# One middle stage of a four-layer kernel: ScalarE put into program order, and the two pairs of batches one turn apart instead of four

## The chip, the cores and the metric

The kernel runs on one core of a Trainium2 chip. A core has five engines that work beside each other and meet through semaphores: TensorE (PE in the profile; PEld is its weight load), VectorE (DVE), ScalarE (ACT), GpSimd (POOL) and SyncE (SP, which here only starts DMA transfers). What is measured is the device time of one execution in microseconds (us); the time of a version is the median of several runs.

## The reference, cut to what matters

Four batches of 512 tokens with 128 features, in float32, pass through four "macaron" layers. Each layer adds half a feed-forward part, an attention part and again half a feed-forward part, each on the normalized x:

```python
x = x + 0.5 * ffn(layernorm(x))
x = x + attn(layernorm(x))
x = x + 0.5 * ffn(layernorm(x))
```

The layers differ in what `ffn` and `attn` are. The change lies between the end of the second layer's attention and the experts of the fourth layer's first feed-forward part. Five parts are computed there:

1. Second layer's second `ffn`: eight small experts with `silu(x wg) * (x wu)`, then `wd`, of which each token uses two with weights made from sigmoid scores, and a shared expert that all tokens use.
2. Third layer's first `ffn`: eight linear experts (`x w_in w_out`), of which each token uses two, with a softmax over the two largest logits.
3. Third layer's `attn`, which is a recurrence: a projection of x to a gate and a hidden part, `g = sigmoid(gate) * silu(hidden)`, then along the tokens `h = 0.9 h + 0.1 g`, then an output projection.
4. Third layer's second `ffn`: as part 2, with the same weights, on the new x.
5. Fourth layer's first `ffn`, its beginning alone: logits, a softmax, the two best experts of each token, and the place of each token among the 512 that an expert takes. The tokens are scattered to those places in DRAM, and the experts then fetch them. In the traces this part is "the third mixture" (f30), the first two being those of the first layer.

## The kernel before, in words

x stays in SBUF for the whole run, in four tiles `xs[b]` of 128 partitions x 4 token tiles x 128 features, one for each batch. Weights of the third layer's experts are folded beforehand: `w_in w_out` of each expert is one 128x128 matrix, all eight in a tile `m`. So one token tile of 128 tokens needs two matmuls of 128x512 (L1419) for all its experts, and VectorE then adds the eight products, each times the gate of its token, to x (L1450, a gating product: 32 for each batch and part, 256 in all).

The stage works on two pairs of batches, 0 and 1, 2 and 3. One Python generator, `behind`, emits the five parts for one pair and yields between steps, and `skewed` takes the generators in turns. The second generator joins in after `lag` turns:

```python
def skewed(gens, lag):
    live = {i: g for i, g in enumerate(gens)}
    r = 0
    while live:
        for i in list(live):
            if r >= i * lag and next(live[i], "end") == "end":
                del live[i]
        r += 1
        yield
```

So the order of the program is a few instructions of pair one, a few of pair two, and so on. What the engines get is not this order for all of them. A planner orders the instructions of each engine by priorities and its own notion of when each is ready. `tc.manual_schedule(engines=...)` takes engines out of that: what is emitted for them inside the block stays in the order of the program. Before the change only GpSimd is in that set here; TensorE, VectorE and ScalarE are ordered by the planner, and SyncE too. Every engine then executes its own list strictly in order, so an instruction that waits holds up all behind it.

The steps, with the lines that the profile names:

- Each part begins with the norm. Statistics on VectorE (L168, L169, one each for every token tile), then GpSimd makes `rs` (L172), `rstd` (L173) and, where ScalarE normalizes, `off` (L176, L177). Normalizing runs on ScalarE (L182) and VectorE (L186), half of the token tiles each in parts 1 to 4; for the third mixture it is all on ScalarE. TensorE transposes (L195), ScalarE copies the result to `nT` (L1124; L321 for the mixture).
- Gate logits: small matmuls (L1133; L330 for the mixture). Routing on VectorE: largest value, one-hot, the rest, the second one (L226 to L239).
- Part 1 (`l1_ffn`): a gu pair of matmuls (L1218, L1219) for each of five blocks of 128 hidden units and each batch; sigmoid on ScalarE (L1222), two products on VectorE (L1223, L1224). For four of the five blocks GpSimd multiplies with the gates of the tokens (L1265), and TensorE projects down (L1253). Then VectorE adds to x (L1271). The gates come as rows: transposed (L1194), copied on ScalarE (L1196), written to DRAM on SP's queue (L1198) and read back spread over the partitions (L1242, `cb_f`). For pair one the norm, logits and rows have been made during the attention before (`l1_early`); pair two makes them here.
- Parts 2 and 4 (`l2_ffn`): logits, the first y matmuls (L1419), routing, two sigmoids for the gates on ScalarE (L1434, L1436), gates on VectorE (L1440 to L1442), then gating products and y matmuls in four rounds.
- Part 3 (`l2_attn`): GpSimd adds the output bias to x (L1055), projections (L1469), two sigmoids (L1471, L1473), three products and the scan on VectorE (L1475, L1476, L1478), output matmuls (L1482), sum (L1483).
- Part 5 (`tokens`): norm, copies, logits, largest value (L344), difference (L346), Exp on ScalarE (L348), routing, running counts (L362), the rank by matmuls with ones (L373 to L379), places (L387 to L409), then the scatters on GpSimd (L416), one for each token tile and each of the two choices: 32. Pair one takes this part with both batches together, pair two with one batch after the other. `f30.experts` (from L434) begins when all scatters have landed.

Of the kernel before, what the change touches and what calls it, by code (L numbers as in the profile page):

```python
# [41 lines left out]
def kernel(ctx: ExitStack, tc: tile.TileContext, a: dict, out: bass.AP):  # L42
# [540 lines left out]
    def padded(pool, i):  # L583
        v = pool.tile([P, NT, NH, SLOT], FP, name=f"vpad{i}", tag=f"vpad{i}", bufs=1)
        nc.gpsimd.memset(v, 0.0)
        nc.gpsimd.memset(v[:, :, :, HD : HD + 1].rearrange("p t h o -> p (t h o)"), 1.0)
        return v
# [499 lines left out]
    def prep_l1():  # L1087
        l1["gate"] = load_T(a["L1_ffn_gate_weight"], E, D, "gate1T")
        l1["wg"] = load_T(a["L1_ffn_w_gate"].rearrange("e i h -> (e i) h"), E * I1, D, "wg1T")
        l1["wu"] = load_T(a["L1_ffn_w_up"].rearrange("e i h -> (e i) h"), E * I1, D, "wu1T")  # L1090
        l1["sg"] = load_T(a["L1_ffn_ws_gate"], D, D, "sg1T")
        l1["su"] = load_T(a["L1_ffn_ws_up"], D, D, "su1T")
        sd = load_T(a["L1_ffn_ws_down"], D, D, "sd1T")
        raw = stage.tile([P, E, I1], FP, name="raw_wd1", tag="raw")
        nc.sync.dma_start(raw, a["L1_ffn_w_down"].rearrange("e h i -> h e i"))
        ps = bank("wd1")
        for c in range(NC):
            nc.tensor.transpose(
                ps[:, c * P : (c + 1) * P], raw[:, 2 * c : 2 * c + 2, :].rearrange("p e i -> p (e i)"), ident
            )  # L1100
        wd = pools["w"].tile([P, NC, D], FP, name="wd1T", tag="wd1T")
        copy(wd, ps.rearrange("p (c d) -> p c d", d=D))
        l1["down"] = [wd[:, c, :] for c in range(NC)] + [sd]

        raw = stage.tile([P, D], FP, name="raw_qk1", tag="raw")
        for i, s in enumerate(("q", "k")):
            nc.sync.dma_start(raw[i * NH * R1 : (i + 1) * NH * R1, :], a[f"L1_attn_W{s}1"])
        ps = bank("qk1")
        nc.tensor.transpose(ps[:, :D], raw, ident)
        qk1 = pools["w"].tile([P, D], FP, name="qk1T", tag="qk1T")  # L1110
        copy(qk1, ps[:, :D])
        l1["factors"] = [qk1] + [load_T(a[f"L1_attn_W{s}2"], NH * R2, D, f"w{s}2T") for s in ("q", "k")]
        l1["wv"] = load_T(a["L1_attn_Wv"], D, D, "wv1T")
        l1["wo"] = load_T(a["L1_attn_Wo"], D, D, "wo1T")
        l1["bo"] = load_row(a["L1_attn_bo"], "bo1")
# [43 lines left out]
    def l1_early(pool, bs, got):  # L1159


        tag = f"f11_{bs[0]}"
        G = len(bs) * NT
        ns = [work.tile([P, NT, D], FP, name=f"n{b}_{tag}", tag="n", bufs=3) for b in bs]
        yield from norms([xs[b] for b in bs], ns, tag, "both", True)
        nTs = []
        for n, b in zip(ns, bs):
            yield
            nT = work.tile([P, S], FP, name=f"nT{b}_{tag}", tag="nT", bufs=4)
            copy(nT, transposed(n, f"{b}_{tag}"))  # L1170
            nTs.append(nT)
            yield
        sc = pool.tile([P, G, E], FP, name=f"sc_{tag}", tag="sc1")
        for x in range(len(bs)):
            yield

            nc.scalar.activation(
                sc[:, x * NT : (x + 1) * NT], scored(nTs[x : x + 1], l1["gate"], f"{x}_{tag}"), AF.Exp, scale=-1.0
            )
        yield  # L1180
        nc.vector.tensor_scalar(sc, sc, 1.0, None, ALU.add)
        nc.vector.reciprocal(sc, sc)
        comb = yield from chosen(pool, sc, G, tag)
        rows = []
        for x, b in enumerate(bs):
            yield
            rows.append(to_rows(work, comb, x, f"{b}_{tag}", "n", 3))
        got[:] = nTs, rows
# [148 lines left out]
    def l1_attn(beside, begun, after):  # L1337
        begin_, fetch_, project_, future, early = begun
        with tc.tile_pool(name="attn1", bufs=2) as pool:
            def begin(b):  # L1340
                if b == 1:
                    vpads[1] = padded(pool, 1)
                if b > 0:
                    yield from begin_(b)

            def fetch(b, g):
                if (b, g) not in early:
                    fetch_(b, g)

            def project(b, g):  # L1350
                return early[b, g] if (b, g) in early else project_(b, g)

            def residual(b, po):
                nc.vector.tensor_tensor(xs[b], po, xs[b], ALU.add)

            attention(pool, "a1_", begin, project, residual, l1["wo"], lambda h: future, after,
                beside(pool), fetch,
            )
# [130 lines left out]
    def prep_l3_ffn(behind):  # L1489
        l3["w"] = yield from moe_weights("L3_ffn", "l3", behind)  # L1490
        l3["gate"] = wpool.tile([P, E], FP, name="gate3", tag="gate3")
        nc.sync.dma_start(l3["gate"], a["L3_ffn_wg"])
# [78 lines left out]
    def whole(parts):  # L1571
        for _ in parts:
            pass
# [11 lines that stand above are left out]
# [19 lines left out]
    pairs = [[b, b + 1] for b in range(0, NB, 2)]  # L1604
# [41 lines left out]
    with tc.tile_pool(name="weights12", bufs=1) as mid:  # L1646
        pools["w"] = mid
        prep_l1()
        with tc.tile_pool(name="raw2", bufs=1) as pool:
            made = prep_l2(pool)  # L1650
            next(made)
            next(made)
            f01.experts(l0["w"], made.send)
            whole(made)
        first = small.tile([P, 1], FP, name="first_sigmoid", tag="first_sigmoid", bufs=1)
        nc.scalar.activation(first, l2["m"][:, 0, 0:1], AF.Sigmoid)
        for b in pairs[0]:
            whole(f01.combine(b))
        with tc.tile_pool(name="ahead1", bufs=2) as ahead:
            vpads[:] = [padded(ahead, 0), None]  # L1660
            begun = l1_begin(ahead)

            def followed(pool, bs):
                if bs[0] > 0:
                    for b in bs:
                        yield from f01.combine(b)
                yield from l1_ffn(pool, 0, bs)
                if bs[0] == 0:

                    yield from begun[0](0)  # L1670
                    for g in range(2):
                        begun[1](0, g)
                        yield
                        begun[4][0, g] = begun[2](0, g)

            with tc.tile_pool(name="ffn10", bufs=2) as pool:
                whole(skewed([followed(pool, bs) for bs in pairs], 10))

            early = []
            with tc.tile_pool(name="gates10", bufs=1) as pool:  # L1680
                l1_attn(
                    lambda _: prep_l3_ffn(xs[0]), begun,
                    lambda b: l1_early(pool, pairs[0], early) if b == 1 else iter(()),
                )

        def behind(pool, bs):
            yield from l1_ffn(pool, 1, bs, early if bs[0] == 0 else None)
            yield from l2_ffn(pool, 0, bs)
            yield from l2_attn(pool, bs)
            yield from l2_ffn(pool, 1, bs)  # L1690
            if bs[0] == 0:

                parts = f30.tokens(bs, l3["gate"], "scalar", pool, apart=True)
                while next(parts, "end") != "end" and next(parts, "end") != "end":
                    yield
            else:
                yield from skewed([f30.tokens([b], l3["gate"], "scalar", pool) for b in bs], 4)

        with tc.tile_pool(name="chain", bufs=2) as pool:
            decay = pool.tile([P, S], FP, name="decay", tag="decay", bufs=1)  # L1700
            nc.gpsimd.memset(decay, 0.9)
            with tc.manual_schedule(engines={mybir.EngineType.Pool}):
                whole(skewed([behind(pool, bs) for bs in pairs], 4))
        pools["w"] = wpool
    prep_l3_attn()
    with tc.tile_pool(name="padded", bufs=1) as pool:
# [52 lines left out]
```

## Time and profile before

Three runs took 1504.37, 1507.65 and 1510.55 us. The profiled execution is a further one:

| | |
|---|---|
| median of the runs | 1507.65 us |
| profiled execution, its own time | 1506.45 us |
| its span in the profile | 1504.7 us |
| mean granted TensorE clock | 0.908 |
| busy over the span | PE 84%, DVE 59%, ACT 46%, POOL 46% |
| busy in 745 to 1002 us (257 us, the part that the edit reorders) | PE 180.0, DVE 167.0, ACT 52.8, POOL 83.7 us |
| granted TensorE clock in 745 to 1002 us | 0.78 |
| chain that ended last, whole span | PE 63%, DVE 13%, POOL 9%, issue 7%, DMA 6% |

The largest groups of the stretch from 745 to 1002 us are, in VectorE, the 256 gating products with 69.6 us; in TensorE, the 128 y matmuls (L1419) with 64.7 us; in GpSimd, the 32 scatters (L416) with 31.1 us and the 16 products L1265 with 20.2 us; in ScalarE, 36 normalizings (L182) with 14.8 us and 20 sigmoids (L1222) with 11.8 us.

How to read it: the busy share of an engine over the whole span says little about this stretch. In a stretch where two engines feed each other, look at the busy time by windows of 10 to 30 us. An engine that is over 0.9 busy in a window sets the pace there; where none is, look at the waits, which name what an engine waited for ("consumer <- engine, tile, line: total us, number of waits, longest us"). In a timeline each line is the start, the duration, the engine, the line of the kernel, the operation, the output and inputs, and in brackets the idle time before it with what ended it. The granted TensorE clock (PEclk) is 1.00 at full speed; the same matmul takes about twice as long at 0.5.

### The profile page before, as it was taken

How to read it: one execution, taken by the hardware profiler on the slowest of the kernel's cores; microseconds unless marked ns; L12 is line 12 of the kernel's file. 1: busy time of each engine (PE TensorE's matmuls, PEld its weight loads, DVE VectorE, ACT ScalarE, POOL GpSimd, SP SyncE). 2: the span in 40 equal slices, each digit the busy share in tenths (PEclk: the TensorE clock that was granted, in tenths of full speed). 3: DMA queues.
4: the chain of work that ended last, by engine and by line, in shares of the span. 5: the costliest groups of instructions: out<-in, count | busy, mean ns of one | idle time of the engine just before them, and what ended most of it. 6: DMA issues, size and time to landing. Idle time of an engine off the chain costs nothing.

```text
span 1504.7 us, 28029 instructions
## 1 busy us (share of the span) xinstructions
PE 1258.4 (84%) x10133; PEld 787.1 (52%) x10133; DVE 893.8 (59%) x3105; ACT 685.7 (46%) x1438; POOL 691.0 (46%) x810
## 2 busy tenths in 40 slices
PE   4788999995979989998999766439599999998394
PEld 4465666674756656676655334227453334333273
DVE  5326766663345657777467766634277787773243
ACT  2135867871443367776621213104245555564041
POOL 5346767872433678876432112554502224212343
PEclk9998999996999999999999776759799999999597
DMA  9420240002413884241130000032105000000223
GB/s 254 114 60 12 80 171 13 9 5 74 137 52 61 228 259 136 93 141 31 32 80 3 1 1 0 29 92 79 56 8 184 9 11 5 15 2 15 78 82 108
DMA packets 100657, 106.15 MB, mean 71 GB/s; under 512 B 9084, under 2 KB 73832, under 8 KB 100520
## 3 DMA queue, kind: packets, MB, share of 16 engines
q1 hardware_dynamic: 89576, 88.01, 20.3%
q0 software_dynamic: 6656, 13.22, 2.5%
q10 hardware_dynamic: 4288, 3.15, 0.8%
q8 instruction: 80, 1.31, 0.3%
q14 instruction: 57, 0.47, 0.1%
HBM read 62.49 MB, written 41.85 MB: 69 GB/s over the span
## 4 chain that ended last, share of the span: by engine, by line
PE 63%; DVE 13%; POOL 9%; issue 7%; DMA 6%; ACT 2%; SPq 0%; POOLq 0%; DVEq 0%; ACTq 0%
PE s_a L621 13%; PE t_a L666 9%; PE o_f L526 5%; PE h_f L490 5%; PE acc_a L688 5%; PE acc_a L826 4%; DVE x L1450 3%; PE t_a L621 3%; PE y_f L1419 2%; POOL disp_f L416 2%; PE ot_a L845 2%; POOL res_f L512 2%; PE gu_f L1218 1%; PE gu_f L1219 1%; PE T_f L195 1%
## 5 line engine op out<-in xcount | busy, mean ns | idle before, releaser
L653 POOL TENSOR_SCALAR sc_a<-sc_a,top_a 128x128 f32<-128x128 f32 (+3 forms) x256 | 275.8, 1092 | 88.0 <-DVE top_a L638 53.8
L621 PE MATMUL s_a<-k_a,q_a 32*128 32x512 f32 (+3 forms) x1536 | 265.1, 539 | 6.0 <-DVE top_a L642 4.8
L710 DVE TENSOR_REDUCE low<-s_a 128x1 f32<-128x512 f32 x256 | 163.0, 684 | 42.8 <-PE t_a L621 31.0
L730 ACT ACTIVATE w_a<-t_a 128x512 f32<-128x512 f32 x240 | 131.6, 596 | 107.1 <-PE t_a L621 69.2
L666 PE MATMUL t_a<-ident,sc_a 128*128 128x128 f32 x1280 | 171.6, 279 | 7.4 <-DVE top_a L642 6.7
L512 POOL DMA_INDIRECT res_f<-y_f,back_f x112 | 106.6, 952 | 140.1 <-ACT y_f L511 92.3
L666 PEld LDWEIGHTS t_a<-ident,sc_a 128*128 128x128 f32 x1280 | 142.8, 143 | 42.6 <-issue 15.8
L621 PE MATMUL t_a<-ql_a,k_a 32*128 32x512 f32 x480 | 157.9, 640 | 0.4 <-DVE low L710 0.3
L655 ACT ACTIVATE sc_a<-sc_a,top_a 128x128 f32<-128x128 f32 (+3 forms) x256 | 134.7, 575 | 16.1 <-DVE top_a L642 15.6
L621 PEld LDWEIGHTS s_a<-k_a,q_a 32*128 32x128 f32 x1536 | 94.7, 186 | 74.5 <-issue 39.0
L675 ACT ACTIVATE w_a<-t_a 128x256 f32<-128x256 f32 (+2 forms) x192 | 94.3, 526 | 70.4 <-PE t_a L666 70.0
L416 POOL DMA_INDIRECT disp_f<-n_f,to_f x96 | 94.8, 988 | 51.5 <-issue 37.2
L526 PE MATMUL o_f<-w_l,h_f 128*128 128x128 f32 (+1 forms) x896 | 111.9, 280 | 3.6 <-ACT h_f L494 3.6
L526 PEld LDWEIGHTS o_f<-w_l,h_f 128*128 128x128 f32 (+1 forms) x896 | 103.9, 186 | 12.6 <-ACT h_f L494 5.6
L490 PE MATMUL h_f<-dT_f,w_l 128*128 128x320 f32 (+1 forms) x256 | 106.6, 555 | 2.8 <-ACT dT_f L468 2.8
L172 POOL TENSOR_SCALAR rs_f<-mv_f 128x4 f32<-128x4 f32 (+1 forms) x23 | 5.3, 231 | 203.4 <-DVE mv_f L169 202.9
L688 PE MATMUL acc_a<-w_a,vpad 128*32 128x128 f32 x2560 | 97.7, 278 | 0.6 <-ACT w_a L675 0.6
L677 ACT COPY w_a<-t_a 128x256 f32<-128x256 f32 (+2 forms) x192 | 93.5, 526 | 5.7 <-PE t_a L666 5.7
L642 DVE CUSTOM_DVE_ANT_0 sc_a<-s_a,table 128x128 f32<-128x128 f32 (+3 forms) x128 | 62.3, 487 | 46.8 <-PE s_a L621 35.2
L642 DVE CUSTOM_DVE_ANT_0 sc_a<-s_a,future 128x128 f32<-128x128 f32 (+3 forms) x128 | 62.4, 487 | 46.3 <-PE s_a L621 39.5
L511 ACT ACTIVATE y_f<-o_f,d_f 128x128 f32<-128x128 f32 (+1 forms) x112 | 38.9, 394 | 105.2 <-DVE o_f L506 93.5
L826 PE MATMUL acc_a<-w_a,vpad 128*32 128x256 f32 x1024 | 82.5, 391 | 2.7 <-ACT w_a L730 2.3
(338 smaller groups left out, 2200.6 us busy)
## 6 DMA issues: line engine op xcount, KB each, us to landing
fac_a<-fac_a_sb SPq DMA_DIRECT2D x36, 256.0 KB
disp_f<-zeros_f SPq DMA_DIRECT2D x4, 2080.0 KB
d_f<-disp_f SPq DMA_DIRECT2D x32, 260.0 KB
w_l<-in_L_ffn_w_dram SPq DMA_DIRECT2D x16, 512.0 KB
cb_f<-rows_f SPq DMA_DIRECT2D x16, 512.0 KB
q_a<-fac_a SPq DMA_DIRECT2D x32, 256.0 KB
k_a<-fac_a SPq DMA_DIRECT2D x32, 256.0 KB
r_f<-res_f SPq DMA_DIRECT2D x16, 256.0 KB
```

Source lines behind the costliest of these rows:

```text
L416: nc.gpsimd.indirect_dma_start(out=self.to[c][i0 + t][:, :], out_offset=bass.IndirectOffsetOnAxis(ap=to[:, c, t : t + 1], axis=0), in_=ns[ ...
L490: nc.tensor.matmul(ps[u][:, :cap], w1[:, e, (c + u) * P : (c + u + 1) * P], dT, start=True, stop=True)
L512: nc.gpsimd.indirect_dma_start(out=self.back[e * per + s][:, :], out_offset=bass.IndirectOffsetOnAxis(ap=back[:m, s : s + 1], axis=0), in_ ...
L526: nc.tensor.matmul(po[:m, s, :], h[:, c, s * P : s * P + m], w2[:, e, c, :], start=(c == 0), stop=(c == NC - 1),)
L621: nc.tensor.matmul(ps[:, n0:n1], q[r : r + SLOT, i * P : (i + 1) * P], k[r : r + SLOT, n0:n1], start=True, stop=True)
L653: nc.gpsimd.tensor_scalar(sc, sc, top, None, ALU.subtract)
L655: nc.scalar.activation(sc, sc, AF.Exp, bias=top, scale=-1.0)
L666: nc.tensor.transpose(ps[:, x * n + j * P : x * n + (j + 1) * P], st["sc", u, i, r0 + x][:, j * P : (j + 1) * P], ident,)
L688: nc.tensor.matmul(st["acc", u][r * SLOT : (r + 1) * SLOT, i * P : (i + 1) * P], vpads[b % 2][:, j, g * 4 + r, :], st["w", u, i, r][:, j * ...
L710: nc.vector.tensor_reduce(st["low", u][:, i, c : c + 1], ps, AX.X, ALU.max, negate=True)
L730: nc.scalar.activation(w, ps, AF.Exp)
L826: nc.tensor.matmul(acc[r * SLOT : (r + 1) * SLOT, n0:n1], vpads[b % 2][:, j, g * 4 + r, :], st["w", u, j, r, half] if ("w", u, j, r, half) ...
```

## The change

ScalarE (`Activation`) joins GpSimd in the set of engines that keep the order of the program, and the second pair of batches joins in after one turn instead of four. No instruction is edited.

```diff
@@ -1699,8 +1699,8 @@
         with tc.tile_pool(name="chain", bufs=2) as pool:
             decay = pool.tile([P, S], FP, name="decay", tag="decay", bufs=1)
             nc.gpsimd.memset(decay, 0.9)
-            with tc.manual_schedule(engines={mybir.EngineType.Pool}):
-                whole(skewed([behind(pool, bs) for bs in pairs], 4))
+            with tc.manual_schedule(engines={mybir.EngineType.Pool, mybir.EngineType.Activation}):
+                whole(skewed([behind(pool, bs) for bs in pairs], 1))
         pools["w"] = wpool
     prep_l3_attn()
     with tc.tile_pool(name="padded", bufs=1) as pool:
```

As GpSimd keeps the order of the program, the second number moves pair two's work on GpSimd three turns forward against pair one's. ScalarE's order is now that of the program as well. TensorE and VectorE are still ordered by the planner, which sees other orders beside them and so gives them other lists too. After the stage, the program is the same.

## The prediction

> **What bounds the stretch now.** The edit acts between about 745 us (third batch leaves the second attention) and 1002 us (first expert of the third mixture can fetch), so I read, in this order, busy time by window there, VectorE's waits in the same window, and the timelines of VectorE, GpSimd and TensorE. The windows first (busy time of each engine, then TensorE's granted clock):
>
> ```profile
> core 0: us, PE busy (x) PEld busy (x) DVE busy (x) ACT busy (x) POOL busy (x), PEclk, DMA share, GB/s
> ...
> 800.00:830.00 30.00, 26.88 (x92) 14.25 (x92) 27.70 (x99) 3.29 (x7) 5.08 (x4) 0.98 0.00 0
> 830.00:850.00 20.00, 15.35 (x56) 9.00 (x57) 11.47 (x51) 7.14 (x17) 7.48 (x10) 0.69 0.00 1
> ...
> 875.00:890.00 15.00, 12.81 (x38) 8.35 (x39) 6.07 (x29) 5.52 (x14) 6.25 (x9) 0.50 0.00 1
> 890.00:920.00 30.00, 18.95 (x51) 9.21 (x49) 27.46 (x103) 2.75 (x4) 0.69 (x2) 0.90 0.00 1
> 920.00:940.00 20.00, 15.73 (x56) 12.09 (x57) 7.84 (x41) 10.04 (x21) 6.72 (x16) 0.50 0.00 0
> ```
>
> VectorE (DVE) is the bound where it is fed (27.7 of 30 us) and stands still in three holes: 8.5 us idle in 830 to 850, 8.9 in 875 to 890, 12.2 in 920 to 940. Its waits say what the holes are:
>
> ```profile
> DVE mx L226 <- PE lg_f L1133: 14.1, 4, 6.3
> DVE mx_f L344 <- PE lg_f L330: 12.6, 3, 5.9
> DVE n_f L186 <- POOL rstd_f L173: 11.6, 5, 3.9
> ```
>
> They are the norm chain: statistics on DVE, rstd on GpSimd, normalizing, transposes, gate logits, back to DVE. In each hole both pairs of batches are in that chain at once, so neither has gating products (L1450) to fill DVE with. Then the tail, on GpSimd:
>
> ```profile
> 962.12 0.22 POOL L172 TENSOR_SCALAR rs_f<-mv_f 128x4 f32<-128x4 f32 x1 [8.05 <-DVE mv_f L169]
> ...
> 979.48 1.12 POOL L416 DMA_INDIRECT disp_f<-n_f,to_f  x1 [3.35 <-ACT nT_f L321]
> ...
> 999.21 0.95 POOL L416 DMA_INDIRECT disp_f<-n_f,to_f  x1 [0.30 <-DMA disp_f<-n_f,to_f]
> ```
>
> At 962.12 batch 2 has its statistics for the third mixture (I call this moment R). The last scatter ends at 1000.16, 38.0 us later, and the experts wait for it. So this stage ends at R plus a tail, and R is DVE's work plus its holes.
>
> **The change, part by part.** No instruction of any weight comes or goes; the orders do. Building both and laying their orders side by side shows: ScalarE, TensorE, VectorE and GpSimd are reordered from here to the third mixture, SP only keeps its order. I walk the new orders by hand with the durations of this trace: L1450 0.26 each (32 in 8.35), L1223 or L1224 0.60, eight statistics 2.1, four normalizings 1.05, a routing (L226 to L1442) 3.1, one batch of the recurrence (L1475, 1476, 1478, 1483) 3.0, rstd 2.0 after the statistics, four ScalarE normalizings 1.65, two nT copies 1.05, gu pair 1.72, sixteen logit matmuls 1.75, eight y matmuls 3.43, GpSimd's L1265 1.25, scatter 1.26.
>
> *To the first gating product.* Pair two's norm now stands on GpSimd behind one L1265 instead of four: done at 757.4, not 761.8. Pair one pays: ScalarE's fourth sigmoid of batch 0 is queued behind the four normalizings that wait for that norm (till 759.05, where its matmul was ready at 754). Pair two's gate rows go out at 771.8 instead of 778.4. They take 9.1 us to come back (778.4 to 787.5 in this trace), and now an L1265 of pair two stands second in GpSimd's queue after batch 1's first one: all of it stalls from 775.1 to 780.9, with three of batch 1's four products behind. Seven L1265 at 1.23 then end at 789.6; x of batch 1 is complete at 791, pair one's n at 796.7 (794.5 before). The gates of batch 0 wait for one more gu pair (g_f is behind that sigmoid), so gating starts at 808.2 where it started at 803.54: 4.7 us lost. But batch 2 is summed at 792 instead of 798.3 and batch 3 at 813 instead of 828.2. Because of the fewer L1223/1224 left to interleave, pair one ends its 64 products at 828.9, against 828.24, though batch 3's statistics and pair two's normalizing are now also behind us.
>
> *From there to pair one's second gating (888.58 before).* DVE has 2.1 statistics, 3.1 routing, 64 L1450 of pair two (16.6; they cover pair one's norm chain and recurrence), 6.0 recurrence of pair one, 2 x 2.1 statistics, 3 x 1.05 normalizing, 3.0 and 2.4 of pair two's recurrence, another routing 3.1, half a set of statistics 1.05: 44.7 us. Its waits: rstd three times (1.9, 1.4, 2.1), the projections of batches 2 and 3 (1.5, 1.9), o_a 1.9, logits 1.1: 11.8, and 2 more for half-clocked matmuls. 828.9 + 58.5 = 887.5. So no time is won on pair one, but pair two's recurrence is done except for one 0.6 us add; in the old order it lies ahead (2 x 3.0).
>
> *Second gating and the third mixture's statistics.* 64 L1450 16.6, add 0.6, statistics 1.05 and 2.1, normalizing 1.05: 21.4, so 908.9 where it was 920.05.
>
> *The third hole.* It stays: pair two's gates (L1434) are queued on ScalarE behind eight normalizings and two copies of pair one, and DVE's L1440 and L344 wait. I take it from the old trace: 920.05 to L344 at 929.49 is 9.4, plus 1.7 to the first product: 920.0. There it was 940.92, because the second pair's routing came after.
>
> *To R.* 64 L1450 16.6, pair one's routing for the mixture between them 4.0, waits for y at half clock 2.5 (as measured, 2.5 idle from 940 to 963), last statistics 0.8: 943.9, against 962.12. Gain 18.2.
>
> *Tail.* Only 6 of pair one's 16 scatters now precede R on GpSimd, 12 before. After R: norm 2.1, 4 scatters 5.05, 0.5, 4 scatters 5.05, norm 2.1, 2 scatters 2.5, small copies 1.0, 8 scatters 10.1, copies 0.9, 8 scatters 10.1: 39.5 us without a gap. What hides the batch 2 chain (normalize, transpose, logits, routing, rank: 14 us after R by the old rows) is the 17.5 us ahead of its scatters. Without that cover it would cost nothing up to 14, then one for one. Old tail 38.0, so 1.5 lost.
>
> Sum: 1000.16 - 18.2 + 1.5 = 983.5, 16.7 us less. Everything after is in the same order. On the profiled execution, 1506.45 us with a span of 1504.7, that gives 1489.8 and 1488.0; it ran 1.2 below the median of the three runs, 1507.65, so the prediction is **1491**.
>
> [...] The clock: after an idle 6.85 us at 833.73 it stayed at half till about 842.5 (9 us), after 922.39 till about 942 (20 us, with gaps). A y matmul is 592 ns at full clock, 1201 at half. [...] My walk leaves TensorE idle from 854.9 to 863.4. [...] I take some 14 us, between. The tables: ScalarE loads one four times in this stretch now (747.54, 927.75, 931.47, 972.91), two fewer after, since pair two's sigmoids precede pair one's Exp. [...]
>
> **Rivals.** *Half the gain:* the holes move instead of closing. Each of my seven waits ends in another engine's queue; if they double (11.8 more), R is 955.7 and the time 1503. For it: three engines are in program order now, in which a late head holds everything. Against: the 64 products really lie beside the other pair's chain. *More gain:* full clock and no y waits, R at 938: 1485. *Slower:* TensorE's clock decides. There are sixteen groups of eight y matmuls; one takes 3.43 at full clock, 6.3 at half, and DVE eats it in 4.2. A half-clocked group so costs 2.1. Eight of them eat the 16.7; from twelve on it is slower by 0.5%; all sixteen (about two and a half in the old trace) lose 28: 1519. For it: the lockstep holes gather TensorE's idleness, the new order spreads it. Against: 0.98 and 0.90 in the windows where y matmuls and gating run side by side. *It doesn't do what it says:* pinning ScalarE alone, at the old lag, changes only a dozen places of its order; the lag does the work. If lag and pin cancel, 1508.
>
> **Chances.** The forecast's own case 0.55 (1486 to 1499), more gain 0.12, half the gain or none 0.20 (a third of it, near 1500 and below, still over 0.5% faster), slower 0.13. 0.5%, 7.5 us, is about what a measurement of this kernel tells from no change: faster 0.55 + 0.12 + 0.06 = 0.73, same 0.14, slower 0.13. The range is 1483 to 1508: it leaves out the slow-clock case and the luckiest end (all y waits gone and both ScalarE loads counted in full), together under 2 in 10.
>
> **What would show it.** Right: DVE over 0.9 busy from 837 to 860 while pair one is in its recurrence; no stretch like 875 to 890; a stall of 8 to 10 us ended by L330's logits near 920; R at 940 to 948; scatters gapless after R, 39 to 40 us. Wrong: R past 955, clock under 0.8 in the y stretches, GpSimd waiting inside the tail, or a cb_f return much over 9 us near 781.

## The result, and the profile after

Eleven runs of the changed kernel have a median of 1494.87 us, eleven of the kernel before 1507.15. The ratio is 0.9941 (95% interval 0.9923 to 0.9959), which is 8.9 us of 1507; the medians lie 12.3 apart. In a later group of runs the ratio was 0.9952 (0.9936 to 0.9968), 7.2 us. The forecast was 1491 against 1507.65, a ratio of 0.989: the direction holds and the time is in the range, but the gain is little more than half of the one forecast.

The profiled execution took 1492.82 us with a span of 1491.1, at a granted clock of 0.913. Two spans of single executions are no good measure of this gain, since they differ in parts that the edit does not touch. So I count the stage by itself: from ScalarE's table load at its head (L1222, 747.5 us before, 741.3 after; up to there every engine has the same list) to the end of the last scatter. That is 252.6 us before and 240.4 after; in a second profile of each, 251.4 and 242.8. Landmarks below are counted from that head.

| us after the head | before, two profiles | forecast | after, two profiles |
|---|---|---|---|
| first gating product of pair one | 56.0, 57.0 | 60.7 | 63.2, 62.5 |
| end of its last of 64 | 80.7, 81.7 | 81.4 | 84.1, 83.4 |
| first product of pair one's second gating | 141.0, 141.8 | 140.0 | 149.4, 148.9 |
| first product of pair two's second gating | 193.4, 194.1 | 172.5 | 180.4, 181.6 |
| R, batch 2's statistics for the third mixture | 214.6, 213.3 | 196.4 | 201.8, 204.2 |
| end of the last scatter | 252.6, 251.4 | 236.0 | 240.4, 242.8 |

The forecast column is the prediction's own walk less 747.5. The windows of the changed kernel, with the same columns as those of before (busy time and count by engine, then the granted clock). They count from the start of the span, and the head of the stage stands 6.2 us earlier here:

```profile
core 0: us, PE busy (x) PEld busy (x) DVE busy (x) ACT busy (x) POOL busy (x), PEclk, DMA share, GB/s
...
830.00:850.00 20.00, 14.56 (x40) 7.19 (x39) 19.62 (x69) 4.29 (x10) 2.79 (x4) 0.91 0.00 0
...
875.00:890.00 15.00, 11.93 (x33) 7.20 (x32) 6.13 (x26) 1.57 (x4) 0.00 (x0) 0.70 0.00 1
890.00:920.00 30.00, 26.80 (x82) 14.39 (x82) 24.58 (x108) 7.50 (x19) 5.47 (x12) 0.83 0.00 0
920.00:940.00 20.00, 13.35 (x36) 6.64 (x36) 18.66 (x85) 1.18 (x2) 6.55 (x10) 0.83 0.07 21
```

One of VectorE's three holes is filled: 830 to 850 went from 11.47 to 19.62 us busy. The one from 875 to 890 is as large as it was, 6.13 of 15 us against 6.07. The third is more than halved and has moved: 920 to 940 went from 7.84 to 18.66, but 5.7 us of idle time, in two pieces, now lie between 915 and 921:

```profile
919.56 0.22 DVE L1440 SCALAR_TENSOR_TENSOR mask<-mask,g_f 128x64 f32<-128x64 f32 x1 [4.56 <-ACT g_f L1434]
920.92 0.22 DVE L344 TENSOR_REDUCE mx_f<-lg_f 128x8 f32<-128x64 f32 x1 [1.14 <-PE lg_f L330]
```

VectorE's waits in the stage, as before: consumer, what it waited for, us in total, times, longest:

```profile
DVE mx_f L344 <- PE lg_f L330: 14.1, 3, 7.0
...
DVE n_f L186 <- POOL rstd_f L173: 7.8, 3, 4.2
DVE hid_a L1475 <- ACT hid_a L1473: 5.2, 1, 5.2
DVE mask L1440 <- ACT g_f L1434: 4.6, 1, 4.6
...
DVE mx L226 <- PE lg_f L1133: 3.4, 2, 2.5
```

The wait for the logits of the linear experts (L226) is down from 14.1 to 3.4 us. Two are new, 5.2 and 4.6 us, and both are waits for sigmoids of ScalarE. GpSimd at the moment R:

```profile
937.16 0.96 POOL L416 DMA_INDIRECT disp_f<-n_f,to_f  x1 [0.31 <-issue]
943.14 0.22 POOL L172 TENSOR_SCALAR rs_f<-mv_f 128x4 f32<-128x4 f32 x1 [5.03 <-DVE mv_f L169]
...
980.70 0.96 POOL L416 DMA_INDIRECT disp_f<-n_f,to_f  x1 [0.30 <-issue]
```

R is at 943.14, six scatters precede it, and from there GpSimd works to 981.66 without a gap over 0.5 us: a tail of 38.5.

### The profile page after: what moved, and what is told of

Read it like the earlier page. It is cut to its first block, busy times and chain, and to the rows that moved or that the text cites. A ratio compares the mean times of both kernels' runs of the same rounds, so it can differ in the third digit from the quotient of the medians.

```text
span 1491.1 us, 28015 instructions
## 1 busy us (share of the span) xinstructions
PE 1254.3 (84%) x10133; PEld 781.2 (52%) x10133; DVE 892.7 (60%) x3105; ACT 682.6 (46%) x1436; POOL 692.1 (46%) x810
## 4 chain that ended last, share of the span: by engine, by line
PE 63%; DVE 14%; POOL 8%; issue 7%; DMA 5%; ACT 2%; SPq 0%; POOLq 0%; DVEq 0%; ACTq 0%
PE s_a L621 13%; PE t_a L666 8%; PE o_f L526 5%; PE h_f L490 5%; PE acc_a L688 5%; PE acc_a L826 5%; DVE x L1450 3%; PE t_a L621 3%; POOL disp_f L416 3%; PE gu_f L1218 2%; PE y_f L1419 2%; PE gu_f L1219 2%; PE o_f L1253 2%; PE ot_a L845 2%; POOL res_f L512 2%
## 5 line engine op out<-in xcount | busy, mean ns | idle before, releaser
L666 PEld LDWEIGHTS t_a<-ident,sc_a 128*128 128x128 f32 x1280 | 141.0, 142 | 41.9 <-issue 16.0
```

The costliest lines, as they stand in the source:

```text
L666: nc.tensor.transpose(ps[:, x * n + j * P : x * n + (j + 1) * P], st["sc", u, i, r0 + x][:, j * P : (j + 1) * P], ident,)
```

## The experiments

The runs were made in four groups, the fourth of one kernel, each beside runs of the kernel before on the same chip (medians of before: 1510.94, 1495.77, 1511.58, 1495.79). Ratios are to those. "Stage" is from one profile each, and two profiles of the same kernel differed by 1.3 and 2.4 us.

### Which half of the edit does it

The lag alone:

```diff
-                whole(skewed([behind(pool, bs) for bs in pairs], 4))
+                whole(skewed([behind(pool, bs) for bs in pairs], 1))
```

> GpSimd alone keeps the order of the program, as before; the second pair comes one turn behind. The stage is counted from ScalarE's table load at its head (L1222, 747.5 us before, 741.3 after) to the end of the last scatter (1000.2 before, 981.7 after): 252.6 us before, 240.4 after. Theory (the lag makes the gain, the order of ScalarE costs a little of it: VectorE's wait of 5.15 us for two sigmoids at 882.5 in the profile after): stage 235 to 241, time 1490 to 1496. Rival (the order of ScalarE makes the gain): stage 250 to 254, time about 1507. Second rival (only both together do): 1500 to 1507.

Measured: ratio 0.9949 (0.9932 to 0.9966), stage 242.4. The order of ScalarE alone, at lag 4:

```diff
-            with tc.manual_schedule(engines={mybir.EngineType.Pool}):
+            with tc.manual_schedule(engines={mybir.EngineType.Pool, mybir.EngineType.Activation}):
```

> ScalarE in the order of the program, the second pair still four turns behind. Theory (the lag makes the gain): stage 250 to 256, time 1505 to 1511, the three holes of VectorE where they were. Rival (the order of ScalarE makes it): stage about 240, time about 1495.

Measured: ratio 1.0002 (0.9981 to 1.0023), stage 251.9. VectorE's waits from its head to R:

```profile
DVE mx L226 <- PE lg_f L1133: 16.3, 4, 6.0
DVE n_f L186 <- POOL rstd_f L173: 12.2, 5, 3.9
```

The old holes are all there. So the lag brings the gain, and ScalarE's order brings nothing that can be measured in the whole, with the lag or without it: 0.9949 and 0.9941 lie in each other's intervals. My addition that it costs a few us is not borne out either: the lag alone was to be at 235 to 241 and was at 242.4. In its profile the waits for L1434 (4.7 us) and L1473 (2.7) are there as well.

In its parts, ScalarE's order does act. At lag 4 it made R later (218.1 us after the head, against 214.6 and 213.3) and the tail shorter (33.8 against 38.0 and 38.1), and the two cancel. With the lag the tail does not depend on it: 38.5 in both kernels.

### What about the lag

No lag, then two turns, both with ScalarE in program order (`, 1))` becomes `, 0))` and `, 2))`). Three turns were not run.

> As the change, but no lag at all. If the gain comes from the pairs standing apart by just so much that one's gating lies beside the other's norm, lag 0 puts both norms side by side again: stage 246 to 256, time 1501 to 1511. If it comes from having pair two earlier whatever the distance, it is as the change or better: stage 237 to 241, 1491 to 1496.

Measured: ratio 0.9932 (0.9907 to 0.9957), stage 242.5. The theory as I had put it, that lag 0 sets both norms side by side, is wrong.

> As the change, but two turns of lag. If the time follows the distance smoothly from one turn (240.4) to four (252.6): stage about 244, time 1497 to 1500. If what decides is where single waits fall in ScalarE's and GpSimd's lists, it can be on either side of both: below 238 or above 250.

Measured: stage 244.2, as the smooth course has it; ratio 0.9989 (0.9971 to 1.0006). By its time this kernel has no gain that can be told from none, so for two turns the stage of one profile stands alone. I come back to that below.

The lag also sets how many of pair one's scatters precede R on GpSimd: 4, 6, 8 and 12 at lags 0, 1, 2 and 4 (ScalarE in program order), with tails of 41.1, 38.5, 36.5 and 33.8 us. An earlier R is paid for in part by a longer tail.

Counting the yields gives an explanation of both stages. A part of the linear experts takes nine turns, the recurrence also nine, and pair two's l1_ffn takes five turns more than pair one's, whose norm was made earlier. So with a lag of four the second pair stands exactly nine turns behind: it begins each part in the turn in which pair one begins the next, and both are in their norms at once, each time. With a lag of 0, 1 and 2 the distance is 5, 6 and 7. To test it I left the change alone up to L1271 and put the old distance behind it:

```diff
             yield from l1_ffn(pool, 1, bs, early if bs[0] == 0 else None)
+            for _ in range(3 if bs[0] else 0):
+                yield
             yield from l2_ffn(pool, 0, bs)
```

> As the change, with three empty turns for the second pair after its L1271, so that it enters the linear experts three turns later. Counting the yields: a part of l2_ffn takes 9 turns (3 for the norm, 1, 1, 4 rounds of gating), l2_attn too 9 (3 and 2 x 3), and the second pair's l1_ffn takes 5 turns more than the first one's, which has its norm and gates ready. So the pairs stand lag + 5 turns apart: 9 before, one whole part, with both norms side by side at every part; 6 after the change; 5 and 7 with lags 0 and 2. This kernel has the change's order to L1271 and the old distance of 9 behind it. Theory (the distance within the part of nine turns decides): holes of 5 to 6 us at L226 come back, stage 249 to 254, time as before to within 4 us. Rival (what gained is that the second pair's own part is done earlier, by 6 and 15 us at its two L1271): stage 240 to 244, time as after the change.

Measured: ratio 1.0001 (0.9990 to 1.0013), stage 250.3, R at 216.5. VectorE's waits to R:

```profile
DVE mx L226 <- PE lg_f L1133: 14.7, 4, 6.7
...
DVE n_f L186 <- POOL rstd_f L173: 10.0, 5, 3.7
```

The wait for the logits is back at 14.7 us (14.1 before, 3.4 after). Having pair two's l1_ffn done earlier is worth nothing by itself; what counts is the distance within a part of nine turns.

### The size of the gain

The changed kernel again, and later the kernel before again, both unaltered.

> The changed kernel unaltered, on the chip of this call, for a second profile of it. Its stage should be 240.4 again within 2 us; the rest of the program behind the experts' first matmul, 500.8 in its first profile and 496.3 to 505.9 in the five others, should follow the time at half clock in it and not the change.

Measured: ratio 0.9952 (0.9936 to 0.9968), stage 242.8, behind the experts' first matmul 491.5.

> The kernel before, unaltered, for a second profile of it, since the size of the gain hangs on one: from the head to the last scatter 252.6 us in its profile, 240.4 and 242.8 in the two of the changed kernel, 11 us less, where the times of many runs say 7 to 9. If its stage is 252.6 again within 1 us, the stage gains 11 and some is given back behind it; if it is 249 to 251, the stage gains what the times say and the first profile was a long one. The rest behind the experts' first matmul should follow its time at half clock, whatever the stage.

Measured: ratio 1.0005 (0.9993 to 1.0017), stage 251.4, behind it 490.4. So the stage gains 8.6 us between these two profiles and 12.3 between the first two, 10.4 on the mean, and the times 7 to 9. That is as near as single profiles allow; that something is given back behind the stage is neither shown nor excluded.

### Where the missing part is

The hole that stayed, in the profile after: the timelines of VectorE, TensorE and ScalarE between 873 and 891 us (start, duration, what; in brackets the idle time before it and what ended it):

```profile
879.27 0.22 DVE L226 TENSOR_REDUCE mx<-lg_f 128x8 f32<-128x64 f32 x1 [2.45 <-PE lg_f L1133]
...
887.69 0.75 DVE L1475 SCALAR_TENSOR_TENSOR hid_a<-proj_a,bin2T,hid_a 128x512 f32<-128x512 f32 x1 [5.15 <-ACT hid_a L1473]
```

```profile
875.81 3.42 PE L1133 MATMUL lg_f<-gate2T,nT_f 128*128 128x8 f32 x16
879.09 6.12 PE L1419 MATMUL y_f<-m,nT_f 128*128 128x512 f32 x8
885.05 1.88 PE L1469 MATMUL proj_a<-nT_a,win 128*128 128x512 f32 x4
```

```profile
886.11 0.69 ACT L1471 ACTIVATE gate_a<-proj_a,bin2T 128x512 f32<-128x512 f32 x1 [13.87 <-PE proj_a L1469]
...
887.55 0.20 ACT L1434 ACTIVATE g_f<-apart_f 128x8 f32<-128x8 f32 x1
```

Batch 3's projection (885.05) stands in TensorE's list behind pair one's sixteen logits and eight y matmuls, most of which run at half clock; its two sigmoids wait 13.87 us for it, and pair one's gates (887.55, their input ready at 881.84) are queued behind those. Two remedies tell whether it is ScalarE's list or TensorE's. First, the projection and its sigmoids directly behind batch 2's, for pair two only (`project` holds L1469, L1471 and L1473 as they were):

```diff
+        if bs[0] > 0:
+            for x, b in enumerate(bs):
+                project(x, b)
         for x, b in enumerate(bs):
             add_row(b, l2["b_out"])
-            ps = pair(f"proj{b}_{tag}")
...
+            if bs[0] == 0:
+                project(x, b)
             yield
```

> As the change, with batch 3's projection and its two sigmoids (L1469, L1471, L1473) put directly behind batch 2's, instead of two turns later behind the first eight y matmuls of pair one. Theory (the miss of my forecast lies there: pair one's gates L1434 wait on ScalarE behind batch 3's sigmoids, these for the projection, this for eight half-clocked y matmuls, 5.15 us of VectorE): second gating 146 us after the head instead of 149.4, R 198 to 199.5 instead of 201.8, stage 236.5 to 238.5. Rival (the y matmuls at half clock, 6.1 us, have to be waited for in any case): second gating and R unmoved within 1 us.

Measured: ratio 0.9913 (0.9890 to 0.9936), stage 234.1, R at 195.6, second gating from 143.7; the median is 7.2 us under the changed kernel's in the same group. TensorE then:

```profile
882.02 1.19 PE L1133 MATMUL lg_f<-gate2T,nT_f 128*128 128x8 f32 x8
883.07 1.10 PE L1419 MATMUL y_f<-m,nT_f 128*128 128x512 f32 x2
884.01 0.95 PE L1133 MATMUL lg_f<-gate2T,nT_f 128*128 128x8 f32 x8
884.82 2.82 PE L1419 MATMUL y_f<-m,nT_f 128*128 128x512 f32 x6
```

Logits and y matmuls take 5.6 us together where they took 9.4. The granted clock is 0.69 from 880 to 884 and 1.00 from 884 to 890. In all three profiles with the early projection (this one and the two below that have it too) the half-clock stretch ahead of these matmuls lasted 3.41 us and 20.48 us at full clock followed; in the five with a lag of one turn and the late projection it lasted 10.24. So the early projection gave two things, a shorter queue ahead of its sigmoids and a faster clock, and how the gain divides between them is not shown.

Second, ScalarE's list is altered and TensorE's is not: batch 3's sigmoids come one turn later, behind pair one's gates.

```diff
+            if b == NB - 1:
+                yield
             gate = pool.tile([P, S], FP, name=f"gate{b}_{tag}", tag="h1", bufs=6)
...
-            yield
+            if b < NB - 1:
+                yield
```

> As the change, with only ScalarE's list altered at one place, beside the few VectorE steps that the planner moves with it: batch 3's two sigmoids L1471 and L1473 stand behind pair one's gates L1434 and L1436 instead of ahead of them; TensorE keeps projection and y matmuls as they are. Theory (the order of the program on ScalarE holds the gates up, not TensorE): second gating 144 to 146 us after the head (149.4 in the first profile of the change), stage 3 to 5 us under the 240.4 and 242.8 of its two profiles: 236 to 239. Rival (the early projection of the run before helped in another way, with TensorE's half-clocked y matmuls or the recurrence): second gating and stage as in the change within 1.5 us.

Measured: ratio 0.9958 (0.9942 to 0.9974), stage 245.9. The second gating begins at 145.2, as the theory has it, and takes 26.2 us instead of 19.6; R is at 207.3. VectorE and TensorE there:

```profile
892.82 1.38 DVE L1450 SCALAR_TENSOR_TENSOR x<-y_f,gates_f,x 128x128 f32<-128x128 f32 x5 [0.89 <-PE y_f L1419]
896.12 0.75 DVE L1478 SCALAR_TENSOR_TENSOR hid_a<-proj_a,bin2T,hid_a 128x512 f32<-128x512 f32 x1 [1.91 <-ACT hid_a L1475]
```

```profile
893.48 1.88 PE L1469 MATMUL proj_a<-nT_a,win 128*128 128x512 f32 x4
899.26 1.94 PE L1485 MATMUL o_a<-wout,hs_a 128*128 128x128 f32 x8 [3.90 <-DVE hs_a L1481]
901.00 5.35 PE L1419 MATMUL y_f<-m,nT_f 128*128 128x512 f32 x10
```

(L1478 and L1485 are the changed kernel's L1475 and L1482.) The gates are early now, but the next y matmuls stand in TensorE's list behind batch 3's output matmuls, those behind its scan, and that behind the late projection. The lag alone shows the same: there too pair one's gates are ahead of batch 3's sigmoids on ScalarE, and by line and tile TensorE's list in the stage is the changed kernel's. Its second gating began at 141.4 us, took 26.7, and R came at 203.9, no earlier than in the changed kernel. So ScalarE's order only decides which instruction shows the wait; the late projection on TensorE is the cause.

### The tail

Ten of pair one's scatters ahead of batch 2's norm on GpSimd, in place of six (each number is how many steps of its generator one turn takes):

```diff
-                while next(parts, "end") != "end" and next(parts, "end") != "end":
-                    yield
+                for n in [2] * 4 + [3, 3, 4] + [2] * 3:
+                    for _ in range(n):
+                        next(parts, "end")
+                    yield
```

> As the change, with ten of pair one's scatters ahead of batch 2's norm on GpSimd where the change has six. GpSimd waits 5.03 us there (937.2 + 0.96 to 943.14), four scatters take 5.06. Theory (the tail is GpSimd's own work without a gap, so that what is done ahead of the norm is gone from it): stage 235.4 to 237, tail 33.5 to 35, time 4 to 5 us under the change. Rival (batch 2's chain of normalizing, logits, routing and rank, 13 to 14 us, then sets when its scatters may start): no gain, the same 38 us tail with a new wait ahead of L413.

Measured: ratio 0.9925 (0.9908 to 0.9942), tail 33.9, R at 205.8, stage 239.7; the median is 2.5 us under the changed kernel's in the same group. GpSimd, the last scatter ahead of the norm and the norm:

```profile
949.30 0.96 POOL L416 DMA_INDIRECT disp_f<-n_f,to_f  x1 [0.30 <-issue]
950.33 0.22 POOL L172 TENSOR_SCALAR rs_f<-mv_f 128x4 f32<-128x4 f32 x1
```

The idle 5.03 us ahead of the norm are gone, and the tail is 4.6 shorter, four scatters less. R was 1.6 us later than in the second profile of the change; up to the first gating product, where both have the same lists, it was already 3.1 us later (65.6 against 62.5). Both altered places together:

> Both altered places in one kernel: batch 3's projection early, and ten scatters ahead of batch 2's norm. If they are independent: R 195 to 198 after the head, tail 33.5 to 34.5, stage 229 to 232, time some 3 to 4 us under the early projection alone. If the earlier R leaves GpSimd no idle time ahead of the norm (pair one's scatters then come too late), the ten delay R and the tail gives nothing: stage 233 to 235.

Measured: ratio 0.9886 (0.9857 to 0.9916), R at 198.3, tail 33.9, stage 232.3. In the ratio they add up (0.9913 and 0.9925 against 0.9952 for the change), and this kernel is faster than the changed one, whose ratios were 0.9941 and 0.9952. The stage is 1.8 us under that of the early projection alone, since the tail is 4.6 shorter and R 2.7 later. Last, pair two's gates ahead of pair one's eight normalizings, which is the second new wait on ScalarE:

```diff
-                for n in [2] * 4 + [3, 3, 4] + [2] * 3:
+                for n in [1, 0, 2, 3, 5, 3, 4] + [2] * 3:
```

> As the run before, and pair one's part of the third mixture is given out in turns of 1, 0, 2, 3, 5, 3 and 4 steps instead of 2, 2, 2, 2, 3, 3 and 4, so that pair two's gates (L1434) stand on ScalarE ahead of pair one's eight normalizings and two copies, not behind. The wait of 4.6 us ahead of L1440 should go. Theory (it is another queue on ScalarE on VectorE's path): pair two's second gating and R 3 to 5 us earlier, stage 225 to 228. Rival (pair one's logits are then late, L344 takes over as the wait and its scatters come behind R): stage as the run before or up to 3 us longer.

Measured: ratio 0.9886 (0.9860 to 0.9913), R at 201.8, stage 235.8. The wait of 4.6 us is gone, but pair one's logits and places come later:

```profile
926.01 0.35 DVE L1450 SCALAR_TENSOR_TENSOR x<-y_f,gates_f,x 128x128 f32<-128x128 f32 x1 [2.57 <-PE y_f L1419]
...
954.40 0.19 DVE L344 TENSOR_REDUCE mx_f<-lg_f 128x4 f32<-128x32 f32 x1 [10.27 <-PE lg_f L330]
```

Pair two's gating begins 6 us earlier and ends only 0.9 us earlier than in the run before, and the wait for batch 2's logits grows from 5.9 to 10.3, since ten scatters that began later now hold up its norm. The rival holds: the ratio is the same and the stage 3.5 us longer.

## Why the prediction was right, and where it was too large

**What bounds, and which half acts.** Right. VectorE's holes were the stage's loss, the lag closes one of them and more than halves another, and ScalarE's order by itself changes nothing in the whole. What I had not seen is why the holes were there: a part of nine turns and a distance of nine.

**To the first gating product.** Forecast a loss of 4.7 us, measured 7.2 and 5.5. The queues that I named (the fourth sigmoid behind four normalizings, GpSimd's stall for `cb_f` to 775.8) are in the trace. Most of the loss goes with ScalarE's order: that alone, at lag 4, has its first product at 63.3, the lag alone at 59.4.

**From there to pair one's second gating.** This is the step that came out too small. From the end of the first gating I forecast 58.5 us: 44.7 of work, 11.8 of waits and 2 for the clock. It took 65.3 and 65.5. In the first of them the named waits are 17.2 us, and the rest, work and short gaps, is 48.1: each is 3.4 over what I had. The largest wait is the term "the projections of batches 2 and 3 (1.5, 1.9)": batch 2's cost nothing and batch 3's 5.15 and 5.6, because it stands behind logits and y matmuls in TensorE's list, and because these ran at half clock (sixteen logits 3.42 us, where those from 842.52 in the trace before took 1.88; a y matmul up to 1201 ns, 592 at full clock). The logits (2.5 for 1.1) and the output matmuls (2.8 for 1.9) grew too.

With the projection moved the same stretch took 58.9 us and R came at 195.6, where the forecast had 58.5 and 196.4. That they lie so near is in part luck: it was 9.8 us of waits and 49.1 of the rest, against 13.8 and 44.7.

**The signs and the rivals.** VectorE was over 0.9 busy from 837 to 860 (21.4 of 23 us), and the tail was gapless. Two signs were not seen: the hole from 875 to 890 stayed, and the stall near 920 was 4.6 us ended by L1434 and 1.1 ended by L330's logits, not 8 to 10. R at 943.14 lies in "940 to 948" by luck: the head is 6.2 us earlier in this profile, and counted from the head the range was 192.5 to 200.5, with R at 201.8. Of the rivals, "half the gain" (1503) lies on the right side of 1491 and named the mechanism, a late head of a queue; but the waits did not double.

**The clock.** The granted clock of the profile after, in windows cut at its changes (busy times, then clock):

```profile
856.70:867.00 10.30, 4.27 (x17) 3.89 (x18) 7.61 (x33) 2.71 (x6) 3.93 (x5) 0.50 0.00 1
867.00:873.80 6.80, 3.68 (x12) 1.37 (x10) 4.86 (x7) 4.14 (x9) 4.83 (x6) 1.00 0.00 0
873.80:884.00 10.20, 10.05 (x30) 7.30 (x31) 3.91 (x22) 0.00 (x0) 0.00 (x0) 0.50 0.01 2
```

TensorE's work began again at 862.73, after 8.26 us idle, and the clock was full from 867.0, 4.3 us later. That is far from the 14 us that I took. In the 6.8 us that followed TensorE was busy 3.68, and then the clock dropped a second time. It stayed at half for 10.2 us in which TensorE was busy 10.05; why is not shown. The sixteen logits and six of the eight y matmuls fell into that stretch. I had weighed one idle stretch and how long the clock stays at half behind it, not a second stretch at half.

My rival of the slow clock (from eight half-clocked groups of y matmuls on) did not come: 22 of the 128 y matmuls ran at half clock, 16 before. That is two groups of eight before, where I had counted two and a half. Their durations, which overlap, add up to 87.4 us against 84.4.

**From the second gating to R.** Part of the loss came back. In the profile after, the third hole was 9.3 us from pair one's statistics (ended at 171.1) to pair two's second gating at 180.4, not the 11.1 that I took from the old trace (9.4 and 1.7), and the second gating to R took 21.4, not 23.9. So R was 5.4 us late, after 9.4 at the gating.

**The tail.** Forecast 39.5 (its terms add up to 39.4), measured 38.5 and 38.6, gapless from R on. What I had passed over is that GpSimd stands idle ahead of R (8.05 us before, 5.03 after): that time was free for scatters, and four of them moved there shorten the tail by 4.6 us. Two of the four table loads went, of 1.28 us each in the trace before (at 931.47 and 972.91), and nothing was to be seen of them. The luckiest end, which my range leaves out, counts both in full; what a load costs beyond its 1.28 us no run shows.

## What to carry to other kernels

Where two streams of work are interleaved by turns, count the turns of a part and the distance of the streams: at a distance of a whole part both are in the same phase here, and VectorE has no work of one to cover the waits of the other (14.1 us for the logits of L226 at nine turns, 3.4 at six). A wait for an engine in program order is followed back to the instruction that is truly late; moving the one that shows the wait moves the wait. And an engine that idles ahead of the last chain's start is the place for that chain's own later work (5.03 us idle here, 4.6 off the tail).

## What the runs showed of the hardware that was not expected

Parts of the program with the same lists on every engine took different times from execution to execution. Up to the head of the stage it was 747.5 us before and 741.3 after, with TensorE at half clock for 81.9 and 71.7 us of it. Behind the experts' first matmul it was 490.4 to 505.9 us in fourteen profiles. Most of that goes with the group of runs, and each group had a chip of its own: 500.2 to 505.9 in the four of the first group, 490.7 to 491.5 in the four of the second, 502.7 to 503.9 in the three of the third, 490.4 in the one of the fourth. The time at half clock does not account for this step: the shortest of the first group has 87.2 us of it and the second group 84.5 to 85.3, 2 to 3 us less for 9 us of time, and the first profile of the kernel before took 496.3 us with only 76.5. Within the first group the two do rise together (500.2, 504.2, 504.8 and 505.9 us with 87.2, 94.6, 98.6 and 103.1 us at half clock). What else differs from chip to chip stays open. Differences of 5 us between single spans say nothing about an edit here.

In the profiles before and after, the stretches at half clock are multiples of 3.41 us (3.41, 6.83, 10.24 and so on), 20 of 21 before and 19 of 20 after; the exception is the last one of each, 19.07 and 18.61 us. What that comes from is not shown. Why the two-turn kernel's ratio (0.9989) shows less than its stage (8 us shorter) would give was not settled; its profiled run, 1506.38 us, was one of the faster of its twenty (median 1510.24).
